# Second attention of a gated two-layer block: routing steps, key transposes and their places

## The chip, the cores and the metric

The kernel runs on one core of a Trainium2 chip. The metric is the device time of one execution in microseconds. Before the change the median of three runs is 2804.81 us (2800.51 to 2809.4). A shorter time is better.

TensorE (PE) multiplies and transposes, VectorE (DVE) and ScalarE (ACT) read its results out of PSUM, GpSimd (POOL) issues the indirect transfers, SyncE (SP) issues the plain ones.

## The reference, cut to what matters

The input `x` has 32 batches of 100 rows of 256, the context 32 batches of 361 rows of 192. Two layers follow each other, each an attention and a mixture of experts, all added to `x` behind a gate:

```python
x = x + tanh(g_xattn[0]) * L0_xattn(layernorm(x), ctx)           # 8 heads
x = x + tanh(g_ffn[0])   * L0_moe(layernorm(x))                   # 8 experts, top 2
x = x + tanh(g_xattn[1]) * L1_xattn(ctx, layernorm(x), mask)      # 4 heads of 64
x = x + tanh(g_ffn[1])   * L1_moe(layernorm(x))                   # 16 experts, top 4
```

The second attention takes the rows of `x` as latents. Its keys and values come from the normalised context and from the latents together, 363+100 positions with padding; queries and keys are normalised per head, the softmax is masked:

```python
q = ln @ Wq.T
k, v = split(concat([xn @ Wkv.T, ln @ Wlkv.T], axis=1))
attn = softmax(where(mask, rmsnorm(q) * scale @ rmsnorm(k).T, -max))
out = (attn @ v) @ Wo.T + bo
```

The router of the second mixture takes sigmoids of 16 logits, keeps the two best of four groups of four, then the four best experts, and scales their weights to a sum of 2.5.

## The kernel before, in words

Everything is float32. The kernel has four stages, one after the other on one core: first attention with its routing, first experts, second attention with its routing, second experts with the final transposes. The change lies in the third stage.

**Batches.** The third stage loops over the 32 batches (`attend1`). It is a pipeline: in batch n it does the scores, softmax weights and values of batch n, the keys and values of the context for n+2 (`context1`), the latents' keys, values and queries for n+2 (`latents1`), the statistics of the context for n+3 (`stats1`), and the transposes of keys and queries for n+1 (`turn1`). `scores1` multiplies transposed queries by transposed keys and leaves the exponentials; `weights1` transposes those (`t`) and copies them out (`aT`, half by VectorE, half by ScalarE); `values1` multiplies them by the values into `o`; `normalise` transposes the reciprocals of the sums (`rT`) and writes the batch's output, `aor`.

**PSUM.** There are four small banks of 512 columns (`bank`) and two pairs of neighbouring banks (`pair`). Scores and the transposed weights use pairs. All the rest takes small banks; `o` keeps one from the first values to `normalise`.

**Routing.** The rows of `aor` are cut anew into 25 tiles of 128. For each tile `residual1` loads the residual `x` (tile `xt`, SP), adds the bias (POOL), multiplies by the output weights (`op`) and takes the statistics. With the fourth tile of a group `route1` follows: normalised rows (`row`), their transposes (`xnT`) and logits (`lg`) for each tile; a chain of small VectorE operations for groups and experts (`first_max`, six times) up to `member` and the weights `w`; then `tile_dispatch`: counts of each expert (`cnt`, two matmuls over `member`), positions and indices (`idx`), and 16 indirect writes of rows into the experts' sorted lists, four a tile (POOL, L279). After that `w` is transposed (`wt`) and multiplied by the second biases (`b`), one tile at a time, added to `xt` and stored by SP.

**The order.** `residual1` and `route1` are generators: each `yield` ends a step. A list `todo` holds them, and `beside1(k)` runs the next k steps; a generator that ends takes no step. `attend1` calls it three times a batch; those places are called slots here: the first before the second half's weights are transposed, the second behind the second half's values, the third behind `normalise`. So TensorE's order is written out by hand: every matmul and transpose of this stage goes through the helpers `mm` (L171) and `tr` (L174), which keep it in the order of the program. The order on VectorE, ScalarE, POOL and SP is laid out by the framework's scheduler when the kernel is built, by what is ready; it also hands out the banks as they come free. Each queue then runs in order.

Of the kernel before, what the change touches and what calls it, by code (L numbers as in the profile page):

```python
# [8 lines left out]
F32 = mybir.dt.float32  # L9
U8 = mybir.dt.uint8  # L10
I32 = mybir.dt.int32
AF = mybir.ActivationFunctionType
# [5 lines left out]
P = 128  # L18
B, S, D = 32, 100, 256
SC, DC = 361, 192  # L20
CJ = 121
# [24 lines left out]
def flamingo_kernel(ctx: ExitStack, tc: tile.TileContext, a: dict, out: bass.AP):  # L46
# [10 lines left out]
    def bank(name):  # L57
        return ps_m.tile([P, 512], F32, tag="m", name=name)

    def pair(name):  # L60
        return ps_s.tile([P, 2, 512], F32, tag="s", name=name)
# [111 lines left out]
    def tr(*args):  # L173
        return tc.keep_in_program_order(nc.tensor.transpose(*args))  # L174
# [582 lines left out]
    with tc.tile_pool(name="p2", bufs=2, reuse_waits="tile") as wk, behind(tables, mark["pe"]):  # L757
# [160 lines left out]
        def turn1(n):  # L918

            kq, rq, mb = ready1.pop(n)  # L920
            kT = wk.tile([P, 2, SK1], F32, tag="kT", name=f"kT1_{n}")
            qT = wk.tile([P, 2 * S], F32, tag="qT", name=f"qT1_{n}")
            for p in range(2):
                ps = bank(f"kT1_{n}_{p}")
                for j in range(Q):
                    m = CJ if j < KL else S
                    tr(
                        ps[:, j * CJ : j * CJ + m], kq[:m, j, p * P : (p + 1) * P], ident[:m, :m]
                    )
                nc.scalar.activation(kT[:, p, :], ps[:, :SK1], AF.Copy)  # L930
            ps = bank(f"qT1_{n}")
            for p in range(2):
                tr(ps[:, p * S : (p + 1) * S], kq[:S, Q, p * P : (p + 1) * P], ident[:S, :S])
            nc.scalar.activation(qT, ps[:, : 2 * S], AF.Copy, scale=gqk)
            made1[n] = kT, qT, kq, rq, mb

        def scores1(n, p, kT, qT, rq, mb, den):
# [55 lines left out]
        def residual1(t):  # L993

            t0 = t // NB * NB
            n = min(NB, NT - t0)
            if t == t0:
                row = wk.tile([P, NB, R1], F32, tag="row", name=f"row1_{t}", bufs=1)
                nc.gpsimd.memset(row[:, :, D + E1 :], 0.0)
                mv = wk.tile([P, NB, 2], F32, tag="mvx", name=f"mvx1_{t}")  # L1000
                rows[t0] = row, mv, []
            _, mv, xs = rows[t0]
            x = wk.tile([P, D], F32, tag="xt", name=f"xt1_{t}", bufs=NB + 1)
            nc.sync.dma_start(out=x, in_=la.acc[t * P : (t + 1) * P, :])
            nc.gpsimd.tensor_tensor(x, x, bo1, ALU.add)
            yield
            ps = bank(f"op1_{t}")
            at = t * P % AR
            for c in range(2):
                mm(ps[:, :D], aor[:, c, at : at + P], wo1[:, c, :], start=(c == 0), stop=(c == 1))  # L1010
            nc.vector.tensor_tensor(x, ps[:, :D], x, ALU.add)
            bs = wk.tile([P, 6], F32, tag="bsx", name=f"bsx1_{t}", bufs=3)
            nc.vector.bn_stats(bs, x)
            nc.vector.bn_aggr(mv[:, t - t0, :], bs)
            xs.append(x)
            yield
            if t < t0 + n - 1:
                return
            yield from route1(t0, n, *rows.pop(t0))

        def route1(t0, n, row, mv, xs):
            rs = wk.tile([P, NB], F32, tag="rsx", name=f"rsx1_{t0}")
            rsqrt(rs[:, :n], mv[:, :n, 1], eps)
            shape = [P, n, E1]

            def small(tag, w=E1):
                return wk.tile([P, NB, w], F32, tag=tag, name=f"{tag}1_{t0}")[:, :n, :]

            sg = small("rt_s")
            for b in range(n):  # L1030
                xr = row[:, b, :D]
                nc.vector.tensor_scalar(
                    xr, xs[b], mv[:, b, 0:1], rs[:, b : b + 1], ALU.subtract, ALU.mult
                )
                tp = bank(f"xnT1_{t0}_{b}")
                for k in range(2):
                    tr(tp[:, k * P : (k + 1) * P], xr[:, k * P : (k + 1) * P], ident)
                xt = wk.tile([P, D], F32, tag="xnT", name=f"xnT1_{t0}_{b}")
                nc.scalar.activation(xt, tp[:, :D], AF.Copy)
                yield  # L1040
                lg = bank(f"lg1_{t0}_{b}")
                for k in range(2):
                    mark["pe"] = mm(
                        lg[:, :E1], xt[:, k * P : (k + 1) * P], wg1[:, k, :], start=(k == 0), stop=(k == 1)
                    )

                mark["act"] = nc.scalar.activation(sg[:, b, :], lg[:, :E1], AF.Exp, scale=-1.0)
            nc.vector.tensor_scalar(sg, sg, 1.0, None, ALU.add)
            nc.vector.reciprocal(sg, sg)

            gm = small("rt_g", 4)
            sg4 = sg.rearrange("p b (r e) -> p (b r) e", e=4)
            nc.vector.tensor_reduce(gm.rearrange("p b r -> p (b r)").unsqueeze(2), sg4, AX.X, ALU.max)
            _, g1 = yield from first_max(wk, gm, revg[:, :n], P, [n, 4], f"1_{t0}_g0")
            nc.vector.scalar_tensor_tensor(gm, g1, -4.0, gm, ALU.mult, ALU.add)
            _, g2 = yield from first_max(wk, gm, revg[:, :n], P, [n, 4], f"1_{t0}_g1")
            nc.vector.tensor_tensor(g1, g1, g2, ALU.add)

            nc.vector.tensor_scalar(g1, g1, 4.0, -4.0, ALU.mult, ALU.add)
            cur = small("rt_c")  # L1060
            nc.vector.tensor_tensor(
                cur.rearrange("p b (r e) -> p (b r) e", e=4),
                sg4,
                g1.rearrange("p b r -> p (b r)").unsqueeze(2).to_broadcast([P, n * 4, 4]),
                ALU.add,
            )
            member = small("rt_mb")
            for t in range(K1):
                _, oh = yield from first_max(wk, cur, rev[:, :n], P, [n, E1], f"1_{t0}_{t}")
                if t == 0:  # L1070
                    nc.vector.tensor_copy(member, oh)
                else:
                    nc.vector.tensor_tensor(member, member, oh, ALU.add)
                if t < K1 - 1:
                    nc.vector.scalar_tensor_tensor(cur, oh, -16.0, cur, ALU.mult, ALU.add)
            w = small("rt_w")
            nc.vector.tensor_tensor(w, member, sg, ALU.mult)
            r = small("rt_r", 1)
            nc.vector.tensor_reduce(r, w, AX.X, ALU.add)
            nc.vector.reciprocal(r, r)  # L1080
            nc.vector.tensor_scalar(r, r, 2.5, None, ALU.mult)
            nc.vector.tensor_tensor(w, w, r.to_broadcast(shape), ALU.mult)
            yield from tile_dispatch(wk, lb, t0, n, w, member, row, tg[:, 3:4], mm)

            tp = bank(f"wt_{t0}")
            for b in range(n):
                tr(tp[:E1, b * P : (b + 1) * P], w[:, b, :], ident)
            wt = wk.tile([E1, NB * P], F32, tag="wt", name=f"wt_{t0}")
            nc.vector.tensor_copy(wt[:, : n * P], tp[:E1, : n * P])
            for b in range(n):  # L1090
                ps = bank(f"b2_{t0}_{b}")
                mark["pe"] = mm(ps[:, :D], wt[:, b * P : (b + 1) * P], b2g, start=True, stop=True)
                nc.vector.tensor_tensor(xs[b], ps[:, :D], xs[b], ALU.add)
                nc.sync.dma_start(out=lb.acc[(t0 + b) * P : (t0 + b + 1) * P, :], in_=xs[b])
                yield
# [3 lines left out]
        def beside1(k):  # L1099

            for _ in range(k):
                while todo and next(todo[0], todo) is todo:
                    todo.pop(0)

        def attend1(n):
            kT, qT, kq, rq, mb = made1.pop(n)
            den = wk.tile([S, H1], F32, tag="den", name=f"den1_{n}")
            es = [scores1(n, p, kT, qT, rq, mb, den) for p in range(2)]
            if n + 2 < B:
                context1(n + 2)  # L1110
            a0 = weights1(n, 0, es[0])
            if n + 2 < B:
                latents1(n + 2)
            beside1(2)
            a1 = weights1(n, 1, es[1])
            o = bank(f"o1_{n}")
            values1(0, a0, kq, o)
            if n + 3 < B:
                stats1(n + 3)
            values1(1, a1, kq, o)  # L1120
            beside1(2)
            if n + 1 < B:
                turn1(n + 1)
            normalise(wk, n, o, den, aor, 2, tr)
            beside1(2)

        alternate(group1(0))
        for n in range(3):
# [108 lines left out]
```

## Time and profile before

| what | value |
|---|---|
| median of three runs | 2804.81 us (2800.51 to 2809.4) |
| the profiled execution | 2807.53 us, of which its span 2805.8 us |
| granted TensorE clock, mean of the span | 0.903 |
| PE busy | 2250.1 us (80%) |
| DVE, ACT, POOL busy | 1134.3, 919.1, 481.7 us |
| first scores of the second attention | 1385.8 us after the span's start |
| PE busy from 1382 to 2127 | 598.42 of 745.00 us, clock 0.85 |

Times inside the span count from its start. A line of the profile names the source line, the engine, the operation and the tiles, as output<-input; a number in square brackets is the idle time of that engine before the instruction, with what ended it. "remote" means that a wait ended for which the profile has no record of who ended it; "issue" that no wait is seen. TensorE's ends of matmuls are modelled by the profiler. A float32 matmul stands as two records, a float32 transpose as one.

### The profile page before, as it was taken

How to read it: one execution, taken by the hardware profiler on the slowest of the kernel's cores; microseconds unless marked ns; L12 is line 12 of the kernel's file. 1: busy time of each engine (PE TensorE's matmuls, PEld its weight loads, DVE VectorE, ACT ScalarE, POOL GpSimd, SP SyncE). 2: the span in 40 equal slices, each digit the busy share in tenths (PEclk: the TensorE clock that was granted, in tenths of full speed). 3: DMA queues.
4: the chain of work that ended last, by engine and by line, in shares of the span. 5: the costliest groups of instructions: out<-in, count | busy, mean ns of one | idle time of the engine just before them, and what ended most of it. 6: DMA issues, size and time to landing. Idle time of an engine off the chain costs nothing. (4 is left out here: it accounts for less than half of the span.)

```text
span 2805.8 us, 31912 instructions
## 1 busy us (share of the span) xinstructions
PE 2250.1 (80%) x10647; PEld 1277.4 (46%) x10647; DVE 1134.3 (40%) x3430; ACT 919.1 (33%) x2484; POOL 481.7 (17%) x461
## 2 busy tenths in 40 slices
PE   7999999999995888886699687876865277777774
PEld 3555555555553555554355344444533144444442
DVE  3344444343434221121566464655554233333332
ACT  3443434433332222222355253443432022222220
POOL 0001010100102122222100202112021333333331
PEclk9998999999997999999799787887877599999996
DMA  6000010100103222224411202111010533333334
GB/s 221 20 21 31 20 31 21 36 29 23 33 15 104 38 38 39 39 37 122 113 31 26 66 25 67 39 52 56 24 49 33 185 62 61 62 61 61 62 61 113
DMA packets 133953, 156.37 MB, mean 56 GB/s; under 512 B 21648, under 2 KB 125280, under 8 KB 133664
## 3 DMA queue, kind: packets, MB, share of 16 engines
q1 hardware_dynamic: 100672, 106.58, 13.3%
q0 software_dynamic: 33120, 47.75, 9.8%
q8 instruction: 88, 1.44, 0.2%
q14 instruction: 73, 0.60, 0.1%
HBM read 96.39 MB, written 57.88 MB: 55 GB/s over the span
## 5 line engine op out<-in xcount | busy, mean ns | idle before, releaser
L658 PE MATMUL gub<-wres,xTb 128*128 x460 | 239.7, 647 | 24.4 <-ACT xTb L633 23.7
L694 POOL DMA_INDIRECT accb<-ysb,xb x115 | 179.5, 1561 | 365.6 <-ACT hTb L680 151.1
L650 PE MATMUL gua<-wres,xTa 128*128 x456 | 210.0, 604 | 1.0 <-issue 0.6
L688 PE MATMUL yb<-w,hTb 128*128 x460 | 135.9, 405 | 90.0 <-DVE hTb L679 89.9
L279 POOL DMA_INDIRECT sorteda<-row,idxa x50 | 48.4, 968 | 836.4 <-DVE idxa L270 698.6
L453 ACT ACTIVATE e<-s,neg,rs 100x361 f32<-100x361 f32 x256 | 164.1, 649 | 52.0 <-DVE neg L450 29.9
L688 PE MATMUL ya<-w,hTa 128*128 x456 | 123.3, 394 | 51.2 <-DVE hTa L679 51.2
L477 PE MATMUL o<-aT,v 121*64 121x100 f32 x1536 | 133.0, 265 | 35.0 <-DVE aT L471 32.0
L449 DVE TENSOR_REDUCE neg<-s 100x2 f32<-100x722 f32 x128 | 116.0, 906 | 107.8 <-PE s L447 105.8
L688 PEld LDWEIGHTS yb<-w,hTb 128*128 128x128 f32 x460 | 80.5, 194 | 158.1 <-DVE hTb L679 110.7
L694 POOL DMA_INDIRECT acca<-ysa,xa x57 | 88.6, 1554 | 335.4 <-ACT ysa L693 321.2
L477 PEld LDWEIGHTS o<-aT,v 121*64 121x64 f32 x1536 | 88.9, 138 | 115.7 <-DVE aT L471 47.8
L658 PEld LDWEIGHTS gub<-wres,xTb 128*128 128x128 f32 x460 | 84.9, 198 | 111.7 <-issue 62.8
L635 DVE SCALAR_TENSOR_TENSOR pickb<-number,exb,xb 128x16 f32<-128x16 f32 x115 | 27.0, 235 | 263.9 <-DMA xb<-sortedb 263.9
L650 PEld LDWEIGHTS gua<-wres,xTa 128*128 128x128 f32 x456 | 87.8, 194 | 91.6 <-issue 85.4
L472 ACT ACTIVATE aT<-t 121x300 f32<-121x300 f32 x128 | 53.7, 420 | 226.7 <-DVE aT L471 224.8
L959 ACT ACTIVATE e<-e,neg,ms 100x463 f32<-100x463 f32 x128 | 97.5, 762 | 92.9 <-DVE neg L957 92.8
L635 DVE SCALAR_TENSOR_TENSOR picka<-number,exa,xa 128x8 f32<-128x8 f32 x57 | 12.9, 227 | 283.5 <-DMA xa<-sorteda 283.4
L447 PE MATMUL s<-kT,q 64*100 64x361 f32 x512 | 127.4, 491 | 0.0
L279 POOL DMA_INDIRECT sortedb<-row,idxb x100 | 96.7, 967 | 176.2 <-DVE idxb L270 133.6
L436 DVE COPY v<-v 121x512 f32<-121x512 f32 x96 | 63.4, 688 | 156.9 <-PE v L434 156.9
L688 PEld LDWEIGHTS ya<-w,hTa 128*128 128x128 f32 x456 | 82.1, 190 | 97.0 <-DVE hTa L679 64.7
(334 smaller groups left out, 4276.3 us busy)
## 6 DMA issues: line engine op xcount, KB each, us to landing
xb<-sortedb SPq DMA_DIRECT2D x115, 144.0 KB
cb<-in_ctxT SPq DMA_DIRECT2D x128, 90.8 KB
ca<-in_ctxT SPq DMA_DIRECT2D x64, 136.1 KB
wres<-in_L_w SPq DMA_DIRECT2D x8, 1024.0 KB
xa<-sorteda SPq DMA_DIRECT2D x57, 136.0 KB
w<-in_L_w SPq DMA_DIRECT2D x8, 512.0 KB
wres<-in_L_W1T SPq DMA_DIRECT2D x16, 256.0 KB
wres<-in_L_W3T SPq DMA_DIRECT2D x16, 256.0 KB
```

The costliest lines, as they stand in the source:

```text
L279: nc.gpsimd.indirect_dma_start(out=L.sorted[:, :], out_offset=bass.IndirectOffsetOnAxis(ap=idx[:, b, k : k + 1], axis=0), in_=row[:, b, :] ...
L436: nc.vector.tensor_copy(v[:, j, :], ps[i][:CJ, :])
L447: nc.tensor.matmul(s[:S, i, :SC], q[r, p, cols], kT[r, p, :], start=True, stop=True)
L449: nc.vector.tensor_reduce(neg, s[:S, :, :SC], AX.X, ALU.max, negate=True)
L453: nc.scalar.activation(e[:, i, :SC], s[:S, i, :SC], AF.Exp, bias=neg[:, i : i + 1], scale=rs[:, b : b + 1], accum_out=den[:, 2 * p + i : 2 ...
L472: nc.scalar.activation(aT[:, 1, :], t[:CJ, 1, : NJ * S], AF.Copy)
L477: nc.tensor.matmul(o[i * DH : (i + 1) * DH, p * S : (p + 1) * S], v[:, j, h * DH : (h + 1) * DH], aT[:, i, j * S : (j + 1) * S], start=(j ...
L650: nc.tensor.matmul(gu[:, m, :], xT[:, k, :], wres[:, bass.ds(o * 2 + (k * 1024 + m * 512), 512)], start=(k == 0), stop=(k == 1),)
L658: nc.tensor.matmul(gu[:, 0, :], xT[:, k, :], wres[:, bass.ds(o * 2 + k * 512, 512)], start=(k == 0), stop=(k == 1),)
L688: mark["pe"] = nc.tensor.matmul(y[:, :D], hT[:, c * P : (c + 1) * P], w2[:, bass.ds(o + c * D, D)], start=(c == 0), stop=(c == nf - 1),)
L694: nc.gpsimd.indirect_dma_start(out=L.acc[:, :], out_offset=bass.IndirectOffsetOnAxis(ap=x.bitcast(I32)[:, D + n_e : D + n_e + 1], axis=0), ...
L959: nc.scalar.activation(e[:, i, :SK1], e[:, i, :SK1], AF.Exp, bias=neg[:, i : i + 1], scale=rp[:, i : i + 1], accum_out=den[:, 2 * p + i : ...
```

## The change

`turn1` transposes the queries first, then all keys into a pair of neighbouring banks, and copies them out with one ScalarE operation in place of two. `attend1` calls `turn1` ahead of the second half's values instead of behind them, runs the second slot between the two, and runs three steps in each slot instead of two. `route1` gets five empty steps ahead of `tile_dispatch` and two behind the copy of the transposed weights, which moves from VectorE to ScalarE and has one buffer instead of two. The residual tile `xt` has seven buffers instead of five.

```diff
@@ turn1
-            for p in range(2):
-                ps = bank(f"kT1_{n}_{p}")
-                for j in range(Q):
-                    m = CJ if j < KL else S
-                    tr(
-                        ps[:, j * CJ : j * CJ + m], kq[:m, j, p * P : (p + 1) * P], ident[:m, :m]
-                    )
-                nc.scalar.activation(kT[:, p, :], ps[:, :SK1], AF.Copy)
             ps = bank(f"qT1_{n}")
             for p in range(2):
                 tr(ps[:, p * S : (p + 1) * S], kq[:S, Q, p * P : (p + 1) * P], ident[:S, :S])
             nc.scalar.activation(qT, ps[:, : 2 * S], AF.Copy, scale=gqk)
+            ps = pair(f"kT1_{n}")
+            for p in range(2):
+                for j in range(Q):
+                    m = CJ if j < KL else S
+                    tr(ps[:, p, j * CJ : j * CJ + m], kq[:m, j, p * P : (p + 1) * P], ident[:m, :m])
+            nc.scalar.activation(kT, ps[:, :, :SK1], AF.Copy)
@@ residual1
-            x = wk.tile([P, D], F32, tag="xt", name=f"xt1_{t}", bufs=NB + 1)
+            x = wk.tile([P, D], F32, tag="xt", name=f"xt1_{t}", bufs=NB + 3)
@@ route1
+            for _ in range(5):
+                yield
             yield from tile_dispatch(wk, lb, t0, n, w, member, row, tg[:, 3:4], mm)
...
-            wt = wk.tile([E1, NB * P], F32, tag="wt", name=f"wt_{t0}")
-            nc.vector.tensor_copy(wt[:, : n * P], tp[:E1, : n * P])
+            wt = wk.tile([E1, NB * P], F32, tag="wt", name=f"wt_{t0}", bufs=1)
+            nc.scalar.activation(wt[:, : n * P], tp[:E1, : n * P], AF.Copy)
+            for _ in range(2):
+                yield
@@ attend1
-            beside1(2)
+            beside1(3)
             a1 = weights1(n, 1, es[1])
             o = bank(f"o1_{n}")
             values1(0, a0, kq, o)
             if n + 3 < B:
                 stats1(n + 3)
-            values1(1, a1, kq, o)
-            beside1(2)
             if n + 1 < B:
                 turn1(n + 1)
+            beside1(3)
+            values1(1, a1, kq, o)
             normalise(wk, n, o, den, aor, 2, tr)
-            beside1(2)
+            beside1(3)
```

## The prediction

> **What bounds the kernel now.** First the page: where the stage sits and what TensorE's clock does in it.
>
> ```profile
> span 2805.8 us, 31912 instructions
> ...
> PEclk9998999999997999999799787887877599999996
> ```
>
> Slices are 70 us; the second attention runs from 1385.8 (first scores) to about 2200, where the clock row falls to 7 and 8. The change touches only this stage, so I cut it into batches: each stretch below begins with the scores (`s<-kT,qT`) of one batch, here 10 to 14 (columns: PE, PEld, DVE, ACT, POOL busy, granted clock, DMA share, GB/s).
>
> ```profile
> 1603.90:1619.90 16.00, 15.59 (x97) 8.73 (x96) 10.83 (x29) 9.25 (x22) 0.59 (x1) 1.00 0.13 28
> 1619.90:1646.70 26.80, 22.75 (x122) 14.51 (x122) 15.16 (x49) 13.28 (x39) 0.60 (x1) 0.83 0.12 32
> 1646.70:1665.50 18.80, 18.23 (x101) 9.88 (x100) 10.27 (x29) 9.62 (x24) 0.59 (x1) 0.88 0.10 24
> 1665.50:1711.20 45.70, 24.77 (x112) 14.59 (x112) 22.34 (x94) 10.50 (x27) 17.44 (x19) 0.68 0.23 76
> 1711.20:1732.80 21.60, 20.19 (x107) 11.22 (x106) 12.95 (x34) 9.58 (x24) 2.32 (x5) 0.88 0.16 42
> ```
>
> A quiet batch is TensorE's: 15.6 of 16.0 busy at full clock. Routing of a group of four tiles costs the rest, over five batches: X (11: norm, logits), Y (12: top-4), Z (13: dispatch), W (14), V (15, 18.4 us, one tile's residual). The cycle repeats from batch 8 to 30. Z's 45.7 is the prize; the PE timeline of its twin, batch 8, shows two losses.
>
> ```profile
> 1549.33 0.66 PE L171 MATMUL cntb<-rt_mb,ones_p 128*128 128x64 f32 x2 [3.08 <-DVE rt_mb L1073]
> ...
> 1552.59 1.01 PE L174 MATMUL wt<-ident,rt_w 128*16 128x128 f32 x4 [2.18 <-DVE preb L256]
> 1555.01 1.19 PE L171 MATMUL b<-b2g,wt 16*128 16x256 f32 x2 [1.42 <-DVE posb L264]
> ...
> 1569.75 1.03 PE L174 MATMUL kT<-ident,kq 121*128 121x121 f32 x4 [5.26 <-issue]
> ...
> 1576.32 0.59 PE L174 MATMUL rT<-ident,recx 100*128 100x100 f32 x2 [5.20 <-issue]
> ```
>
> Loss one is 3.08+2.18+1.42 = 6.7 us: routing's matmuls stand in TensorE's queue before VectorE has made their inputs. Loss two falls in POOL's 16 scatters (L279, 0.96 each, one every 1.27 us, 1557.0 to 1577.1). All engines, same batch:
>
> ```profile
> 1569.27 0.76 DVE L1093 TENSOR_TENSOR xt<-b,xt 128x256 f32<-128x256 f32 x2 [7.05 <-remote]
> ...
> 1575.71 0.56 ACT L930 ACTIVATE kT<-kT 128x463 f32<-128x463 f32 x1 [12.92 <-remote]
> ```
>
> The transposes that this copy waits for stand at 1563.87 to 1564.49, yet it starts 11 us later. In the five bursts inside the loop TensorE's completions come on time until about 5.7 us after the first scatter, then one to three between 10 and 19, the rest at 22.8: some 17 us in which almost nothing passes. Back to quiet: which bank the transposes get.
>
> ```profile
> 1414.97 0.76 ACT L856 ACTIVATE ln<-lnT,lnl 128x100 f32<-128x100 f32 x2 [0.61 <-PE lnT L174]
> ...
> 1415.78 1.05 PE L174 MATMUL kT<-ident,kq 121*128 121x121 f32 x8
> ```
>
> **The change, part by part.**
>
> *Transposes earlier, keys in a pair.* Two copies of 0.556 (128x463) become one of 926 columns. Between 200 columns (0.42 with scale, 0.34 without) and 463 the slope is 0.8 ns a column, so about 0.95: ACT saves 0.15. Scores now wait for the whole copy, but 16 value matmuls (0.92) and the reciprocals' transposes (0.25) lie between. Gone: scores<-qT, 0.37 a quiet batch, and rT<-kT, 0.15 to 0.24. New: qT's transposes follow lnT at once and need one of four small banks, which o, two cs and lnT hold. The first is free when ACT ends `ln`, 1415.73, just where kT starts today because the values (0.91) lie before it. So qT waits 0.85, and behind it in TensorE's queue stand kT's transposes, the second values and the next scores. Net per quiet batch 0.85-0.37-0.2 = +0.3 (0 to +0.8). Where a tile's residual delays the aT copies, the second values wait 0.29+0.67 today; that cover is now given by turn1, and V goes 18.4 to about 17.3: -1.1.
>
> *Three steps a slot, seven empty ones.* Counting yields, a group was 23 steps at 6 a batch and is 30 at 9. Load, residual and the first normalised transposes of X now share one slot, with no value matmuls between. Batch 6 today:
>
> ```profile
> 1509.09 1.35 DVE L1032 TENSOR_SCALAR row<-xt,mvx,rsx 128x256 f32<-128x256 f32 x4
> ...
> 1509.53 0.44 PE L174 MATMUL xnT<-ident,row 128*128 128x128 f32 x2 [0.99 <-DVE row L1032]
> ```
>
> The residual's product ends at 1503.6. Behind it come VectorE 0.42+0.43, the square sums' reduction (1.49) that is ready first, 0.17, ACT 0.30+0.21, and a row's 0.4: the row is there at about 1507.1, so TensorE waits 3.5 (2.1 if nothing cuts in, 5.9 if all does as today). X: +3.5, minus today's 0.99 at that place and the 0.96 on aT, +0.85 for qT, minus 0.6 (the two waits above), +0.2 (two logits wait for a copy queued behind the 0.95 one: 0.7 and 0.5, today 0.5 each), +0.6 (the fourth logits move here from Y), and +1.7 for half a clock stretch: batch 12 lost 2.2 us (18.8-16.0-0.6) to 0.12 x 18.8 = 2.3 us of clock, so a 6.8 us stretch at half costs up to 3.4, of which I take half, since TensorE idles in it anyway. X +4.3 (2 to 6.5).
>
> [...]
>
> *The five empty steps.* From the last logits to `cntb` it was 6 steps of 6 a batch and is 9 of 9 (lg3 in X's third slot, counts in Y's third): one batch before and after. VectorE's chain between (1530.2 to 1549.2 in batch 8, 19 us, of which some 9 its own) is as long, so the wait on members stays: 3.08 to 3.4 today, I take 2.5 (0 to 3.4), now at Y's end. Y: -0.6 (logits) +0.3 +0.5 (counts) +2.5 = +2.7. The waits of wt and b, 2.18 and 1.42, are covered: ten us of scores and context lie between.
>
> *The scatters.* They are not split: one step still issues all 16. From counts to the first scatter it was 6.6 us in batch 8 and 5.7 in 13, with 3.4 of other VectorE work between (1.46+1.23+0.67) that is no longer there, but 2.9 of the scores' reductions that are: the first scatter comes about 5 us into Z instead of 21. TensorE's completions stick from 5+5.7 to 5+22.8 = 27.8. At 10.7 it has done scores, context and the latents' products. What the window lets through is bounded by two answers. Everything: Z ends 2 us after it, 29.8. Nothing: t 0.93, o twice 1.8, cs 0.75, lnT 0.25, qT and kT 1.1, b2 1.8, rT 0.25, a residual 0.87 are left, 7.8 at full clock and 13.7 if the clock stays near half: 41.5. In today's window about thirty matmul records complete (o 16, b 4, kT 8, qT 2); thirty from 10.7 on are wt, the first b2, t and the first o, which leaves 5.5. Today the clock is back 6.6 us after the window (1586.5); in that time 3.8 is done and 1.7 follows at full clock: 27.8+8.3 = 36.1, the value I take as nearest to that row. Z: 45.5 (mean of five) to 36.1 = -9.4.
>
> [...]
>
> *W* loses one of two residuals to Z, and part of its half clock: 21.7 to 20.0, -1.7. *Covered at nothing:* the weights' copy moves from VectorE (0.67) to ACT (121x400 takes 0.50), in the window where ACT idles 13 us; without the idle it costs 0.6 a group. Two more `xt` buffers let SP load three residuals early; SP waits 0.7 for such a buffer in the burst, with stores behind it, and the context behind those is not used until ten us later. On POOL the bias additions (L1005, 0.73) move behind an earlier burst and are needed at Z's third slot, after it. Order on engines other than TensorE is laid out when the kernel is built and may shift: inside the bounds.
>
> Sum: 5 x (4.3+2.7-9.4-1.7) = -20.5; four V and batches 2 to 4, 7 x -1.1 = -7.7; quiet 0, 1, 5, 10: +1.2. Total **-27**. The tail behind batch 31 keeps its chain (10.95 and 18.07 us waits): 0, -4 to +2. The profiled execution took 2807.5 (span 2805.8, 1.7 around it) and would be 2780.5; it lies 2.7 over the median of the runs, 2804.8, so the median becomes **2778**.
>
> **Rivals.** *Burst on top of attention, slower.* In Z the window now meets scores, weights and keys, whose results all come back to TensorE. If it starts before t's copies are through, TensorE stands from 6 to 28 and then has 10.5 us of work at half clock: Z 46, total 2778+5 x 9.9 = 2827. For: TensorE is in order, two or three completions per window. Against: ten us of work need no answer. It decides from Z = 41.5, where 5 x 5.4 eats the 27. *Burst passed through:* Z 29.8, 2778-5 x 6.3 = 2746; for it, kT's bank no longer waits for b2 additions (9.6 us in batch 18). *Nothing gained:* Z about 40 to 43, 2797 to 2813. *Scatters innocent:* completions are late for another reason, which does not move with the burst; then Z = 16.3 + 3.2 of routing's matmuls = 19.5, total 2778-5 x 16.6 = 2695; the late completions stand in every one of five bursts, and in no other batch. [...]
>
> **How the numbers follow.** A run of this kernel can tell about 0.3%, 8.4 us, from no change. Forecast and its near side 0.45, passed through 0.15, innocent 0.03: faster 0.63. Nothing gained 0.12. Slower 0.25. The forecast's own range is 2755 to 2797 (Z 31.5 to 40). For 8 in 10: down to 2740, which is Z 29.8 with half of the counts' wait gone too, leaving out innocent and some of passed through; up to 2820, most of slower.
>
> **What would show it.** Right: quiet batches 16.0 to 16.5 with qT waiting on `ln`; xnT of X waiting about 3.5 on `row`; `cntb` still waiting, wt and b not; first scatter about 5 us into Z; Z near 36. Wrong: counts without a wait (then Y gains 2.5 each), Z over 41.5, or quiet batches over 17, which alone would cost 0.7 x 32 = 22 us.

## The result, and the profile after

The changed kernel takes 2766.23 us (median of four runs, 2756.29 to 2768.29) where the kernel before, on the same chip, takes 2802.66 (four runs, 2792.6 to 2809.4): ratio 0.9856, 95% interval 0.9831 to 0.9882. Taken again beside the experiments it was 2768.28 against 2795.4: 0.9889, 0.9856 to 0.9921. So it is faster by 27 to 36 us; the forecast was 2778, -27. The chance of 0.63 stood on the right side, and 2766 lies inside the range of 2740 to 2820.

A session is a group of kernels run together on one chip, the kernel before among them, and every ratio is against that one. The kernel before had a median of 2795 to 2810 us in three sessions, here called *late*, and of 2711 to 2713 in two others, called *prompt*, after what TensorE's completions do behind a burst of scatters (two in a row lie up to 6.4 to 8.6 us apart in the bursts of the trace of before, and 4.1 at most in the first session's traces); the forecast and its measurement are from a late one.

The page of the changed kernel, its span and TensorE's clock in 40 slices:

```profile
span 2763.1 us, 31877 instructions
...
PEclk9998989998998799999699888987887699999996
```

The span is 42.7 us shorter. The loop of the second attention, from its first scores to those of batch 31, is 693.6 us instead of 741.2: -47.6. The stage began 6.7 later, from what lies ahead of it and was not changed, and the rest is 1.8 shorter. Cut into batches as before, 10 to 14 (columns: PE, PEld, DVE, ACT, POOL busy, granted clock, DMA share, GB/s):

```profile
1598.50:1614.80 16.30, 15.45 (x98) 8.72 (x96) 10.30 (x26) 9.70 (x23) 0.60 (x1) 1.00 0.11 28
1614.80:1644.40 29.60, 24.13 (x128) 15.87 (x126) 15.63 (x50) 13.42 (x39) 0.59 (x1) 0.80 0.10 28
1644.40:1665.30 20.90, 18.52 (x101) 9.95 (x100) 18.64 (x75) 10.26 (x24) 0.59 (x1) 0.88 0.10 22
1665.30:1701.00 35.70, 24.02 (x113) 14.62 (x112) 13.88 (x48) 10.46 (x24) 18.30 (x21) 0.71 0.32 105
1701.00:1718.20 17.20, 16.35 (x103) 9.50 (x102) 12.07 (x33) 8.93 (x20) 2.43 (x4) 1.00 0.12 32
```

Batch 11 (X) and 12 (Y) grew by 2.8 and 2.1, batch 13 (Z) fell from 45.7 to 35.7, and batch 14 (W) from 21.6 to 17.2 with its clock back at 1.00. The first of the 16 scatters now leaves 3.4 us into Z, not 20.6; all of them lie inside Z as before. The PE timeline of the same batches shows which waits are left:

```profile
1612.55 0.39 PE L174 MATMUL qT<-ident,kq 100*128 100x100 f32 x2 [0.85 <-ACT ln L856]
...
1630.19 0.66 PE L174 MATMUL xnT<-ident,row 128*128 128x128 f32 x2 [4.04 <-DVE row L1030]
...
1664.73 0.43 PE L171 MATMUL cntb<-rt_mb,ones_p 128*128 128x64 f32 x2 [1.53 <-DVE rt_mb L1071]
...
1675.62 0.60 PE L174 MATMUL wt<-ident,rt_w 128*16 128x128 f32 x4
1678.03 0.69 PE L171 MATMUL b<-b2g,wt 16*128 16x256 f32 x2 [1.81 <-issue]
...
1692.58 0.59 PE L174 MATMUL qT<-ident,kq 100*128 100x100 f32 x2 [9.87 <-ACT ln L856]
```

The quiet batch pays 0.85 at `qT`, X pays 4.04 at the first normalised transposes, Y 1.53 at the counts, `wt` waits for nothing. In Z the wait on the keys' second bank and the one on the copy of the keys are gone, and one of 9.87 stands at `qT`, on a bank that `ln` has to leave. The groups of the keys' copies say the same for the whole kernel (busy, mean ns | idle of ScalarE before them), first before:

```profile
L930 ACT ACTIVATE kT<-kT 128x463 f32<-128x463 f32 x64 | 33.4, 555 | 99.1 <-remote 79.5 <-PE kT L174 19.1
```

and after:

```profile
L932 ACT ACTIVATE kT<-kT 128x926 f32<-128x926 f32 x32 | 30.1, 942 | 9.6 <-PE kT L174 9.5
```

One copy of 926 columns takes 0.942 where two took 1.11 (forecast 0.95). What went is ScalarE's idle time before it: 79.5 us of it ended "remote" before, some 16 a group, and none after.

### The profile page after: what moved, and what is told of

Same layout as the page of the kernel before. It is cut to its first block, busy times and chain, and to the rows that moved or that the text cites. A ratio compares the mean times of both kernels' runs of the same rounds, so it can differ in the third digit from the quotient of the medians.

```text
span 2763.1 us, 31877 instructions
## 1 busy us (share of the span) xinstructions
PE 2250.0 (81%) x10647; PEld 1283.0 (46%) x10647; DVE 1130.8 (41%) x3423; ACT 925.6 (33%) x2459; POOL 486.0 (18%) x461
## 5 line engine op out<-in xcount | busy, mean ns | idle before, releaser
L658 PE MATMUL gub<-wres,xTb 128*128 x460 | 246.1, 662 | 23.9 <-ACT xTb L633 23.0
```

The source lines that it names most:

```text
L658: nc.tensor.matmul(gu[:, 0, :], xT[:, k, :], wres[:, bass.ds(o * 2 + k * 512, 512)], start=(k == 0), stop=(k == 1),)
```

## The experiments

The question was what made Z shorter. The prediction's answer is that the burst of scatters leaves earlier; the rival answer is that the keys are transposed and copied ahead of the work whose banks wait. Each expectation names its own theory A and its rival. Means over the five groups, in us; first part late sessions, second part prompt ones. Neither the kernel before nor the changed kernel has a trace from a prompt session:

| kernel | X | Y | Z | W | sum |
|---|---|---|---|---|---|
| before (the forecast's profile) | 24.8 | 18.5 | 45.5 | 21.7 | 110.5 |
| after | 28.3 | 21.1 | 35.9 | 17.5 | 102.8 |
| slots_234 | 26.7 | 21.1 | 37.2 | 18.1 | 103.1 |
| turn_alone_2 | 25.2 | 18.9 | 36.1 | 24.2 | 104.4 |
| scatters_apart | 29.2 | 21.0 | 18.0 | 19.4 | 87.6 |
| all_three | 26.8 | 20.3 | 17.9 | 21.2 | 86.2 |
| | | | | | |
| steps_alone, steps_alone_2 | 28.9, 28.3 | 21.7, 21.1 | 24.7, 23.4 | 20.6, 20.3 | 95.9, 93.1 |
| turn_alone | 24.5 | 18.8 | 29.9 | 18.0 | 91.2 |
| place_alone | 25.1 | 18.8 | 29.4 | 18.2 | 91.5 |
| keys_first | 29.2 | 21.0 | 23.7 | 19.2 | 93.1 |

**First session (prompt; before 2713.33, 22 runs).** *steps_alone*: the kernel before with everything of the change but `turn1` and its place; all three slots get 3 steps.

```diff
-            x = wk.tile([P, D], F32, tag="xt", name=f"xt1_{t}", bufs=NB + 1)
+            x = wk.tile([P, D], F32, tag="xt", name=f"xt1_{t}", bufs=NB + 3)
...
+            for _ in range(5):
+                yield
             yield from tile_dispatch(wk, lb, t0, n, w, member, row, tg[:, 3:4], mm)
...
+            nc.scalar.activation(wt[:, : n * P], tp[:E1, : n * P], AF.Copy)
+            for _ in range(2):
+                yield
...
-            beside1(2)
+            beside1(3)
...
```

> The routing part alone: three steps a slot, the empty steps, wt on ACT, seven xt buffers; turn1 and its place as before. Theory A (the gain comes from starting the scatters some 17 us earlier in Z and covering the 6.7 us of routing waits): Z stays near 36 us, the kernel near 2777 us, ratio about 0.991, some 26 of the 36 us. Theory B (Z is shorter because the keys are transposed and copied before the window in which completions stick): without turn1 ahead Z goes back to 43 us or more, X keeps its new wait of 4 us on the normalised rows, and the kernel is at 2805 us or slower.

Measured: 2730.0, ratio 1.0065 (1.0042 to 1.0088). Slower by 17 us. Z is 24.7, which neither theory had, so this run could not decide between them.

*turn_alone*: the other part alone, `turn1` as in the change and this in `attend1`, with 2 steps a slot.

```diff
-            values1(1, a1, kq, o)
-            beside1(2)
             if n + 1 < B:
                 turn1(n + 1)
+            beside1(2)
+            values1(1, a1, kq, o)
```

> The transposes alone: one pair, one copy, queries first, ahead of the second values; routing as before with two steps a slot. Theory A: batches with a tile's residual lose their 1.0 us wait on aT, quiet ones gain 0.3 us on qT's bank, Z stays near 45 us; kernel near 2793 us, ratio 0.996. Theory B: Z falls to about 37 us, the kernel to 2755 to 2765 us.

Measured: 2695.02, ratio 0.9941 (0.9920 to 0.9962), -18. Z is 29.9, again neither 45 nor 37.

*keys_first*: the changed kernel with the eight transposes of the keys and their copy ahead of the queries'.

```diff
-            ps = bank(f"qT1_{n}")
...
             ps = pair(f"kT1_{n}")
...
+            ps = bank(f"qT1_{n}")
...
```

> The changed kernel with the keys' transposes (which take a pair, not a small bank) ahead of the queries'. Theory A (qT waits only because it is the first to ask for a small bank after lnT): the 0.85 us wait goes from quiet, Y and V batches, and in Z the eight key transposes are done inside the 9.9 us wait; 20 to 28 us less than the changed kernel, near 2742 us, ratio 0.978 to the kernel before. Rival (the wait only moves, to rT or to the scores, which then wait for the queries' copy queued last on ACT): within 8 us of the changed kernel, 2758 to 2774 us.

Measured: 2707.76, ratio 0.9994 (0.9963 to 1.0024). Quiet batches 5 and 10 fell to 15.48 (16.28 in the trace of after). The changed kernel itself was not run in the first session, so what the order is worth can't be read from the total. But the four kernels of the session can be set side by side: the steps cost 17 us without the transposes and 13 with them (2707.76 against *turn_alone*, with the keys first), and the transposes bring 18 without the steps and 22 with them.

*scatter_twice*: the changed kernel with each burst of the second routing issued a second time into a spare list, 32 scatters.

```diff
-        for b in range(n):
+        twice = [L.sorted, spare] if L.nm == "b" else [L.sorted]
+        for to, b in [(to, b) for to in twice for b in range(n)]:
...
-                        out=L.sorted[:, :],
+                        out=to[:, :],
```

> The changed kernel with each of layer b's dispatch scatters issued a second time, into a spare DRAM tensor that nothing reads: bursts of 32 instead of 16. Theory A (TensorE's completions stick as long as POOL issues scatters): each burst's window grows by 16 x 1.27 = 20 us, Z goes from 36 to about 56 us, and with the tail's burst the kernel is 110 to 125 us longer, near 2885 us. Rival (the completions are late for a reason that does not go with the scatters): Z stays near 36 us; only the tail, where the row's next writer waits for the scatters, is 20 us longer: near 2787 us.

Measured: 2730.46 in one run, Z 24.4 against 23.7 in *keys_first*, the nearest kernel of that session. The loop is 15 us longer (655.4 to 640.4), what follows it 19. Batch 15 alone is 13 longer (30.5 against 17.4); its waits name a load, for which VectorE stood still:

```profile
DVE bs L815 <- DMA xb<-acca: 14.8, 1, 14.8
...
PE q L171 <- DVE kq L879: 11.2, 1, 11.2
```

What stands there is a wait of 14.8 us for a load, not one for TensorE's completions; why the load came late these rows do not show. Theory A priced a burst by its length, and here twice the length left Z where it was. Here the forecast's mechanism was absent: in the bursts of the loop no two completions of TensorE in a row lie more than 4.1 us apart in any of the four kernels, where it is 6.4 to 8.6 in the trace of before. The kernel before ran 89 us below the first measurement, so the kernels of the first session were not the reason; whether the session was, was open.

**Second session (late; before 2795.4, nine runs).** *after_again* and *before_again* are the two kernels unchanged.

> The changed kernel as it is, beside the kernel before on this chip. The first comparison gave 0.9856 on a chip where the kernel before took 2803 us and where TensorE's completions stuck behind the scatters in every trace; the chip of the first four experiments ran the kernel before in 2713 us and no burst stuck there. Theory A (the gain is the burst moved earlier, out of the way of the part of Z that needs answers): where bursts stick (before near 2800) the ratio is 0.985 again and Z is 36 us; where they do not stick (before near 2713) the burst's place is worth nothing, Z is 23 to 25, X is 29 and Y 21.5 as in the version with the keys first, and the ratio lies between 0.995 and 1.003. Rival (the gain is the pairs of banks and the better packing, whatever the chip): 0.985 on both.

Measured: 0.9889 (0.9856 to 0.9921), Z 35.8. Late, and the gain is there, as both theories had it for such a session.

> The kernel before as it is, for a trace of it on this chip. Theory A: if this chip is like that of the first four experiments, Z is near 30 us (as where the transposes alone were moved, 29.5 to 30.3) instead of 45.5, with cntb, wt and b still waiting 2 to 3 us each, X 24.5, Y 18.8, and completions of TensorE come within 2 us of each other through the burst; if it is like the first chip, Z is 45.5 and the completions stick from 5.7 to 22.8 us after the first scatter. Rival (the 90 us between the chips lie elsewhere, in the first attention or in the experts): the second attention's loop is 741 us long on both chips.

Measured: 2790.19 in one run, Z 44.5, loop 732.8. Its PE timeline in batch 13 shows loss two of the prediction, larger than in batch 8 of the first trace:

```profile
1687.60 1.03 PE L174 MATMUL kT<-ident,kq 121*128 121x121 f32 x4 [6.53 <-issue]
1689.73 0.59 PE L174 MATMUL qT<-ident,kq 100*128 100x100 f32 x2 [1.10 <-issue]
1695.45 0.60 PE L174 MATMUL rT<-ident,recx 100*128 100x100 f32 x2 [5.12 <-ACT kT L930]
```

*slots_234*: the changed kernel with 2, 3, 4 steps in the slots.

```diff
-            beside1(3)
+            beside1(2)
             a1 = weights1(n, 1, es[1])
...
-            beside1(3)
+            beside1(4)
```

> The changed kernel with 2, 3 and 4 routing steps in the three slots of a batch instead of 3, 3 and 3. In X the load and the residual stay in the first slot and the first normalised tile's transposes go to the second, behind the first value matmuls and the next batch's transposes. Theory A (X is 4 us longer than before because TensorE waits 4.04 us for row at the first normalised transposes): that wait falls under 1.5 us, X falls by 2.5 to 4 us, five times, so 12 to 20 us less than the changed kernel on the same chip (ratio to it 0.993 to 0.996), less whatever the fourth step costs in the last slot. Rival (X is longer because its steps come faster than VectorE makes their inputs, wherever they stand): the wait moves to the next step (xnT of the second tile or the logits) and X changes by less than 1 us.

Measured: 2764.93, 0.9888 (0.9864 to 0.9913), no different from the change, where 12 to 20 us less were expected. The wait of `xnT` in batch 11 fell from 4.04 to 1.29, as its theory A has it, and X by 1.6 to 2.2 (2.5 to 4 expected). But Z took 1.3 back and W 0.4 to 0.6: the wait at `qT` grew.

```profile
1628.71 0.41 PE L174 MATMUL xnT<-ident,row 128*128 128x128 f32 x2 [1.29 <-DVE row L1030]
...
1686.18 0.59 PE L174 MATMUL qT<-ident,kq 100*128 100x100 f32 x2 [13.50 <-ACT ln L856]
```

*scatters_apart*: the changed kernel with four scatters at a time in the program, the second products of the tiles between them.

```diff
+            send(0)
...
+            for b in range(1, n):
+                for _ in range(4):
+                    yield
+                second(b - 1)
+                yield
+                send(b)
...
```

Here `send` makes the indices of one tile and issues its four scatters, and `second` does the product with the second biases, its addition and its store.

> The changed kernel with the sixteen scatters of a group issued four at a time, five steps apart, with the second products of each tile between them, instead of sixteen in one step. Theory A where bursts stick: four scatters take 5.1 us of POOL, as long as the completions come on time after the first scatter of a burst of sixteen (5.7 us), so none or almost none stick, Z falls from 36 to 22 to 26, W rises by 1 to 2 for the products it takes over, and the kernel is 40 to 55 us faster than the changed one. Theory A where bursts do not stick: within 8 us of the changed kernel. Rival (a completion sticks behind every single scatter by a fixed time, about 17 us over 16, so 1.06 each): the same sum is paid over two batches, and the kernel is within 8 us of the changed one on either chip.

Measured: 2701.87, 0.9664 (0.9636 to 0.9692), 66 us below the changed kernel; 40 to 55 were expected. Z and W of the last whole group but one:

```profile
1877.10:1894.40 17.30, 16.45 (x103) 9.26 (x102) 12.28 (x45) 10.02 (x23) 1.50 (x2) 1.00 0.12 25
1894.40:1913.50 19.10, 17.45 (x103) 9.51 (x102) 11.68 (x32) 9.91 (x24) 12.86 (x15) 1.00 0.44 144
```

Same scatters, same session, and the clock is at 1.00 through both. On POOL they do not leave four by four: in every group the first four start so late, 16 to 18 us into Z, that the second four follow without a pause. The trace has eight, four and four, and Z holds little more than the first (POOL 1.50 in the first line). The residual batches behind, which now hold the last four scatters, rose from 17.1 to 19.7. The rival, a fixed toll for each scatter, is out. That the stall hangs on how many follow each other fits, but the run also moves the first scatters to the end of Z and spreads the second products, and these were not taken apart; the place alone does not free a burst of sixteen, which sticks 3.4 us into Z as well as 20. Behind sixteen, most often three or four of TensorE's completions come in a heap, 22 to 23 us after the first scatter leaves and 2 to 3 us behind the end of the last.

**Third session (late; before 2809.52, nine runs).** *turn_alone_2* is the kernel of *turn_alone* again.

> Only the transposes of the change: the next batch's transposes ahead of the second values, the queries first and the keys in two neighbouring banks with one copy; routing stays at 2 steps a slot, without empty steps, so the sixteen scatters leave some 20 us into Z as before. It was 0.9941 of the kernel before on the chip where no burst sticks. Theory A (the two parts pay on different chips: the transposes some 18 us on any chip, the earlier burst 15 to 25 us only where bursts stick): on a chip where the kernel before takes about 2800, Z stays at 43 to 46 us, V is 17.1, and the ratio is 0.993 to 0.997, so the changed kernel's 0.987 needs the steps too; on the chip of 2713 the 0.994 repeats. Rival (the transposes are the whole gain, the steps none): 0.987 on the sticking chip, with Z under 40.

Measured: 2769.22, **0.985** (0.983 to 0.987). This is the whole gain of the change, and here the prediction's answer falls: Z is 36.1 although the burst leaves 20.4 us into it (batch 13). Batch 13 of one and the same kernel, prompt first, then late:

```profile
1634.60:1665.00 30.40, 23.13 (x116) 13.65 (x114) 21.80 (x94) 10.50 (x26) 8.36 (x9) 0.78 0.20 62
```

```profile
1654.30:1692.00 37.70, 26.28 (x113) 15.66 (x112) 21.24 (x92) 10.38 (x25) 13.93 (x15) 0.67 0.22 70
```

The PE timeline of the prompt one from the transposes on:

```profile
1661.24 0.96 PE L174 MATMUL kT<-ident,kq 121*128 121x121 f32 x8
1662.13 1.13 PE L171 MATMUL b<-b2g,wt 16*128 16x256 f32 x4
1663.19 0.91 PE L171 MATMUL o<-aT,kq 121*64 121x100 f32 x16
...
1664.98 1.80 PE L171 MATMUL s<-kT,qT 64*100 64x463 f32 x8
```

and of the late one:

```profile
1681.54 1.75 PE L174 MATMUL kT<-ident,kq 121*128 121x121 f32 x8
1683.22 2.07 PE L171 MATMUL b<-b2g,wt 16*128 16x256 f32 x4
1685.22 1.60 PE L171 MATMUL o<-aT,kq 121*64 121x100 f32 x16
...
1690.90 1.21 PE L171 MATMUL b<-b2g,wt 16*128 16x256 f32 x2 [3.56 <-issue]
1692.05 3.15 PE L171 MATMUL s<-kT,qT 64*100 64x463 f32 x8
```

Both run all eight key transposes in one piece, behind 0.64 us of waiting at most, and the second values close behind. The late one takes 1.75 us for the key transposes and 1.60 for the second values where the prompt one takes 0.96 and 0.91, at a granted clock of 0.67 over the batch against 0.78, and stands 3.56 at the last `b`, with no wait recorded (it needs a small bank). The order before stood 6.53+1.10+5.12 = 12.8 us still at that place. What the keys' second half waited for is named in the first trace of before, in batch 18:

```profile
DVE xt L1093 <- remote: 10.2, 1, 10.2
PE kT L174 <- DVE xt L1093: 9.6, 1, 9.6
```

The transposes needed a small bank that a residual addition (`xt`) had to leave, and that addition itself stood 10.2 us. The record does not name what it waited for. In batch 13 of *before_again* the products `b` that it adds end at 1680.5 and it starts at 1687.12, so a late completion of TensorE fits.

*all_three*: scatters apart, keys first and slots of 2, 3, 4 together.

> The changed kernel with the scatters four at a time (2702 on the sticking chip, 0.966 of the kernel before, against 0.988 for the change), the keys' transposes ahead of the queries' (quiet batches 15.5 instead of 16.3 where it was tried) and the routing steps 2, 3 and 4 in the three slots. Theory A: the three add up, since none meets the others' place: quiet and residual batches 0.7 us shorter in some 16 batches, 10 us; X 2.3 us shorter five times, 11 us, which is kept now that Z no longer waits for the burst; so 2680 where the kernel before takes 2795 (0.957 to 0.962), and near 0.98 on the chip where nothing sticks. Rival (what the slots save in X is given back in Z, as in the slots' own run, and the keys ahead of the queries delay the scores, as their 0.999 on the other chip against 0.994 for the transposes alone may show): within 6 us of 0.966 on the sticking chip.

Measured: 2688.36, 0.9558 (0.9531 to 0.9584), 121 us below the kernel before and the fastest of the late sessions. The forecast of 2680 to that kernel's 2795 is 0.959, so the three bring together at least what was expected of their sum. In two groups W still takes 24.3 and TensorE waits 5.0 at `qT` (batches 14 and 24). The first two fours of scatters had run together there, eight in a row, but so they had in the other three groups, which have no such wait; what sets the two apart is open.

**Fourth session (prompt; before 2711.21, 21 runs).** *place_alone*: the kernel before with nothing but the place of `turn1`.

```diff
+            if n + 1 < B:
+                turn1(n + 1)
+            beside1(2)
             values1(1, a1, kq, o)
-            beside1(2)
-            if n + 1 < B:
-                turn1(n + 1)
```

> The kernel before with one thing of the change: the next batch's transposes stand ahead of the second values and of the slot of routing between. Keys first, one bank for each half with its own copy, and 2 steps a slot are as before. Where bursts stick, the transposes with the pair of banks gave 0.985, the whole change's gain, with the burst still 20 us into Z. Theory B (the place does it: ahead of the second products the transposes need no bank that waits for a residual addition, so TensorE works on through the window instead of waiting 6.5 us for the keys' second bank and 5.1 for their copy): Z 36 to 39, V near 17.3, and 0.985 to 0.990 on a sticking chip, 0.994 to 0.998 where nothing sticks. Rival (the pair does it: one copy and one wait instead of two): Z over 42 and a ratio of 0.995 or more on a sticking chip, within 0.3% of 1 where nothing sticks.

Measured: 2701.91, 0.996 (0.9934 to 0.9986), -9, Z 29.4 and V 17.4. So without the pair the place brings half of the 18 us of *turn_alone*, or more: the two intervals overlap. The session was prompt, so what the place does against the late completions was not measured.

*steps_alone_2* is *steps_alone* again.

> The other half of the change alone: 3 steps a slot, the empty steps, the weights' copy on ScalarE and two more buffers of xt; the transposes' place, order and banks as before. It was 1.0065 where no burst sticks. On a sticking chip: theory B (two remedies for one stall, so either alone takes most of it): the burst starts 4 us into Z, Z is near 36, X 29 and Y 21.5 as in the other run, the sum of X, Y, Z and W is 107 against 110.5, ratio 0.992 to 0.996. Rival (the parts add, and the steps bring nothing): Z stays at 40 or more, since the keys still wait for a bank and for their copies, and the ratio is 1.000 to 1.006.

Measured: 2724.24, 1.0048 (1.0028 to 1.0068), +13, prompt once more. The steps alone were not seen in a late session. In prompt ones a good part of their cost is one batch: batch 19, behind the third burst, takes 27.6 here and 28.2 in *steps_alone*, where W is 18.4 to 19.5 in the other groups. TensorE waits there for exponentials, whose maxima VectorE makes, and VectorE for a load:

```profile
1798.97 1.95 PE L174 MATMUL t<-ident,e 100*121 100x100 f32 x8 [7.00 <-ACT e L959]
```

```profile
DVE bs L813 <- DMA xb<-acca: 9.1, 1, 9.1
```

SP issued that load late: it had stood 14.8 us for a mask tile (`mb`) that POOL makes, and POOL was at its scatters until then. The prediction had put SP's waits in the burst at nothing.

## Why the prediction was right, and where it was not

The total held: -27 was forecast, -36 and -27 were measured. The loop alone gained more than the sum had for it, 47.6 in the first pair of profiles and 39.2 in the second (732.8 to 693.5). Most terms of the sum held, by the first profile of after: quiet 16.3 (forecast 16.3), V 17.15 (17.3), X 28.3 (29.1), Y 21.1 (21.2), Z 35.9 (36.1), the tail behind batch 31 the same (67.8 us against 67.9 from its scores to the last burst). The waits stand where they were put: `qT` 0.85, `xnT` 4.04 (3.5), counts 1.53 (2.5), none at `wt`, 1.81 at `b` (covered, it was said); the first scatter leaves 3.4 us into Z (5).

Two terms were mis-sized, and with X they make the 20 us by which the first loop beat the sum. W gave -4.2 a group and not -1.7: the working for Z let the clock return before Z ends, and W was charged half a clock stretch all the same; its clock is 1.00. Batches 2 to 4 gave -7 and not -3.3, of which 3 is the profile of before, where two of the three had run long (58.4 us in all; 55.4 in *before_again*). One reading was a little off and changes nothing: in the five bursts of before two to four completions come between 10 and 19 us, not one to three.

**The step that failed, as far as the runs show, is the cause of Z.** Under *the scatters* the prediction has Z fall by 9.4 because the burst starts 5 us into Z instead of 21. *turn_alone_2* has the burst at 20 and Z at 36.1, so the early burst is not needed for it. The other edit is enough: the transposes ahead of the second values, with the keys in a pair of banks, to which the sum gave -1.1 in V, +0.3 in quiet batches, small terms in X and Y and nothing in Z. Whether the steps without the transposes would shorten Z in a late session too was not measured. The fact was on the page and was read: "kT's bank no longer waits for b2 additions (9.6 us in batch 18)" stands under the rival *burst passed through*, as an argument for it, where it should have been a term of its own. The two waits shown there for batch 8, 5.26 and 5.20, stood in plain sight.

What the steps with their earlier burst add to the transposes is the difference between after and *turn_alone_2*, traces of two late sessions: W -6.7, Z -0.2, X +3.1, Y +2.2, -1.6 a group or 8 us in five, which the two ratios (0.9856 and 0.9889 against 0.985) can't tell from nothing. In prompt sessions the steps are a loss, +13 and +17 us, where the transposes gain 18. So that Z came out at 36 was in part luck: the sum credited the 9 us to the early burst and left out an edit that takes them by itself, and had the two effects added, Z would have come out far below 36. The cost in X and Y was credited rightly.

The rivals. *Burst on top of attention* did not come: Z has one stall of 9.87 at `qT` and ends at 36, not 46; nor was the burst *passed through* (29.8), nor *nothing gained* (40 to 43). *Scatters innocent* (Z 19.5) comes nearest to the prompt sessions (Z 23 to 25 in kernels with the steps), yet not as an effect of the change, since the kernel before is 2711 there too.

What a burst of the same scatters goes with differs between the sessions: in a prompt one 32 of them left Z at 24.4, against 23.7 with 16 in *keys_first*, and in a late one *scatters_apart* came 66 us below the changed kernel. What the late traces show is completions that come late; what holds them back no run shows.

**What stays open** is what makes a session late. It is not the kernel, and not the chip by itself, since a chip of the same number ran the third session late and the fourth prompt. One more trait goes with it: the page's list of DMA issues has a time to landing for the scatters in the prompt traces and none in the late ones. Prompt, then late, the same kernel:

```profile
sortedb<-row,idxb POOLq DMA_INDIRECT x100, 2.5
```

```profile
sortedb<-row,idxb POOLq DMA_INDIRECT x100
```

So late traces lack records of these landings. They lack some of TensorE's own completions too, 6 to 25 of 573 to 612 in the loop, where the prompt traces lack 2 at most. That is too few to make the heaps, though a gap inside a burst may hold a missing record; and the waits of TensorE and the times of the runs are no matter of records.

## What to carry to other kernels

Look, for every place where an engine stands still, at what the next instruction needs, a bank or an answer, before asking what made the answer late: putting eight transposes where no bank waits for an answer, with a pair of banks for them, brought as much here in a late session as that and the earlier burst together. When two edits act on one stall, take each by itself before crediting either. Try indirect writes in small groups between other work, and look on POOL how they really leave: eight, four and four instead of sixteen took 66 us of 2768 off in a session where bursts hurt, and with the keys first and slots of 2, 3 and 4 the kernel came to 0.9558 of the one before.

## What the runs showed of the hardware that was not expected

The same kernel can run 3% apart for a whole session: 2711 to 2713 against 2795 to 2810 for the kernel before. In the one kernel with a trace of both kinds all of the difference is in one stretch: outside the loop of the second attention *turn_alone* and *turn_alone_2* differ by 0.1 us (spans 2697.6 and 2765.9, loops 633.6 and 701.8), and of the 68 us inside it Z and W hold 62. There stand the stall behind the bursts of scatters and a lower clock (0.67 against 0.78 in the batch above). A shortened wait did not keep the clock up: X of *slots_234* has no single wait over 1.32 us in batch 11 and a clock of 0.85 there, near the 0.80 of the change with its wait of 4.04.
